# A graph network of four layers: group sums copied out of PSUM by ScalarE, and a written instruction order in the attentions

## Chip, cores and metric

The kernel runs on one core of one Trainium2 chip. The metric is the time of one execution on the device in microseconds (us). Before the change the median of three executions was 2805.52 us (2800.92 to 2822.27).

## The reference, cut to what matters

Four layers follow one another on 3327 nodes with 512 features each; an adjacency matrix of 3327 x 3327 says which node sees which. Every layer has the form x = x + layer(h, adj) with h = relu(layernorm(x)). Layers 0, 2 and 3 are graph attentions with 8 heads of 64 features:

```python
Wh = h @ W                                   # per head
e = leaky_relu(s_i[:, None] + s_j[None, :])  # two scores per node and head
e = where(adj > 0, e, NEG)
out = softmax(e) @ Wh
```

Layer 0 puts a batch norm over the nodes and a relu behind it, layers 2 and 3 an elu. Layer 1 is a SAGE layer: the mean of the neighbours' h, two products with weights that are combined, a relu.

## The kernel before

**Tiling.** Nodes are padded to 26 blocks of 128. A setup (0 to about 405 us) reads the adjacency, projects for layer 0 and builds, for each of 52 groups of 64 target nodes, the list of source nodes that any of them sees. The matrix is sparse, and lists have fixed lengths (CAPS): 22, 15, 13 chunks of 128 source rows for the first groups, 5 for 21 of the last. There are 359 chunks in all.

**A projection** writes one table row per node: for each head the 64 projected features times the exponential of the source's score, that exponential itself as a 65th column, and eight more columns with the exponential of the score times -0.8. The target's factor goes to r_dram. A leaky-relu softmax then needs no exponential per edge: its weight is the maximum of a target's and a source's factor (mx), times the 0/1 mask (wgt), and the 65th column gives the softmax's sum.

**An attention** (attend, L1000) goes through the groups in units of two or three chunks, 135 units a layer. For a unit:

- GpSimd gathers the chunks' rows by an indirect DMA each (L995) into rows, which has six buffers of one unit.
- In layer 0 alone, VectorE takes the adjacency bits of the group out of the rows (on, L1058), and ScalarE makes the mask of them (L1064), which the later layers use again.
- VectorE computes mx in PSUM (L1067) from r_bc, the group's factors spread over the partitions by TensorE (L1024), and the gathered columns; then wgt in SBUF (L1074, three buffers).
- TensorE multiplies wgt with the rows, head by head, into facc, one PSUM bank with two buffers (L1086). Four heads lie side by side on each half of the partitions.

When a group's last unit is through, group_end (L1027) divides by the sums: VectorE takes a reciprocal for each half of the partitions (rd, L1041), reading PSUM, and ScalarE does eight multiplications out of PSUM (L1044) into fhp, or in layer 0 into bn_y. After two groups a block of 128 nodes is whole. In layers 2 and 3 finish() (L1110) then loads x (fin_x), ScalarE takes an exponential and subtracts one, VectorE does two operations (L1118, L1119), and the result goes out by a DMA on ScalarE's queue (L1120).

**Beside an attention** other work goes on, a step at each tick(), called once a unit behind the unit's matmuls. Layer 0 has beside(): products of SAGE weights, and later a matmul per block for the batch norm's mean. Layer 2 has the projection of layer 3 (class Following): norm() makes the layer norm of a finished block in three steps on ScalarE and VectorE; rest() has four steps with transposes, score products (p_sd), the feature product (p_wh), exponentials, and writes to r_dram and the table. Its PSUM has one bank in layer 2, which transposes, p_sd and p_wh use in turn. The SAGE layer drives the same class for layer 2, with two banks. Layer 3 starts when the whole table of layer 3 is written.

**What sets the order.** The kernel is written in Tile: the program gives tiles, buffers and dependences, and a planner orders the instructions of each engine by the time at which its own cost model says that they are ready, with the program's order as priority. [...] The program puts group_end one unit (LATE) behind a group's last unit; where its instructions come to stand is the planner's choice.

Of the kernel before, what the change touches and what calls it, by code (L numbers as in the profile page):

```python
# [29 lines left out]
AF = mybir.ActivationFunctionType  # L30
ALU = mybir.AluOpType
AX = mybir.AxisListType
PSUM = bass.MemoryType.PSUM
# [21 lines left out]
UNIT = 3  # L55
LATE = 1
SUNIT = 2
SROWS = 8
SAHEAD = 2
RB = 2  # L60
SMALL = 53.0
# [584 lines left out]
class Following:  # L646
# [51 lines left out]
    def rest(self, c, hx):  # L698
# [15 lines left out]
        nc.scalar.activation(V[:, :, F : F + 1], sd[:, :H].rearrange("p (h o) -> p h o", o=1), AF.Exp)  # L714
        nc.scalar.activation(row[:, H * (F + 1) :], sd[:, :H], AF.Exp, scale=-0.8, bias=self.cs["down"])  # L715

        rr = pp.tile([H, P], F32, name="r_row", tag="r_row", bufs=2)
        nc.vector.tensor_scalar(rr, sd[:H, P : 2 * P], -SMALL, SMALL, ALU.max, ALU.min)  # L718
        yield True
        wh = self.psum.tile([P, D], F32, name="p_wh", tag="p_ps", bufs=self.pb)  # L720
        for kc in range(KC):
            nc.tensor.matmul(wh, hT[:, kc, :], self.Wt[:, kc, :], start=(kc == 0), stop=(kc == KC - 1))  # L722
        nc.scalar.activation(rr, rr, AF.Exp, scale=0.8, bias=self.cs["down"][:H])
        n = P // GB
        nc.sync.dma_start(
            self.r_dram[c * n : (c + 1) * n, :, :].rearrange("g h i -> h g i"), rr.rearrange("h (g i) -> h g i", i=GB)
        )
        yield True
        for h in range(H):
# [237 lines left out]
def sparse(ctx: ExitStack, tc: tile.TileContext, t: dict, out: bass.AP, WA, ls, cs, idx, rdeg, first):  # L967
# [32 lines left out]
    def attend(layer, table, r_dram, finish, tick=lambda: None, home=None):  # L1000
# [6 lines left out]
        for g in range(ls.G):  # L1007
            mine = list(ls.batches(g, UNIT))
            units += [(g, k0, n, i == 0, i == len(mine) - 1) for i, (k0, n) in enumerate(mine)]
        late = []  # L1010
        with tc.tile_pool(name=f"fatt{layer}", bufs=2) as ap, tc.tile_pool(
            name=f"facc_ps{layer}", bufs=2, space=PSUM
        ) as aps:
            hps, rbs, accs = {}, {}, {}

            def spread(g):


                if g >= ls.G:
                    return  # L1020
                rr = ap.tile([1, H * GB], F32, name="r_one", tag="r_one", bufs=3)
                nc.sync.dma_start(rr, r_dram[g : g + 1, :, :].rearrange("g h i -> g (h i)"))
                rb = aps.tile([P, H * GB], F32, name="r_bc", tag="r_bc", bufs=RB)
                nc.tensor.matmul(rb, ones[0:1, :], rr, start=True, stop=True)  # L1024
                rbs[g] = rb.rearrange("p (h i) -> p h i", i=GB)

            def group_end(g):  # L1027
                b, u = divmod(g, PG)
                if u == 0:
                    if home is None:  # L1030
                        hp_ = ap.tile([P, D], F32, name="fhp", tag="hp", bufs=2)
                        hps[b] = hp_
                    else:
                        hps[b] = home[:, b, :]
                hp, acc = hps[b], accs.pop(g)
                o0 = u * GB
                for v in range(PG):
                    src = acc[v * GB : (v + 1) * GB, : H // PG * (F + 1)].rearrange("p (q x) -> p q x", x=F + 1)
                    rd_ = ap.tile([P, H // PG, 1], F32, name="rd", tag="rd", bufs=4)
                    rd = rd_[v * GB : (v + 1) * GB]  # L1040
                    nc.vector.reciprocal(rd, src[:, :, F : F + 1])  # L1041
                    for q in range(H // PG):
                        h = q * PG + v
                        nc.scalar.mul(hp[o0 : o0 + GB, h * F : (h + 1) * F], src[:, q, 0:F], rd[:, q, :])  # L1044
                if u == PG - 1:
                    finish(b, hps.pop(b), ap)

            spread(0)
            for at, (g, k0, n, begins, ends) in enumerate(units):
                gi = ap.tile([P, UNIT, width], I32, name="rows", tag="rows", bufs=6)  # L1050
                gt = gi.bitcast(F32)
                for k in range(n):
                    gather(gi[:, k, :], table, k0 + k)
                mk = mask[:, k0 : k0 + n, :]
                if layer == 0:
                    nw = GB // WB
                    on = ap.tile([P, UNIT, nw, WB], U16, name="on", tag="on")
                    nc.vector.tensor_tensor(  # L1058
                        on[:, :n],
                        gi[:, :n, ROW:].bitcast(U16)[:, :, g * nw : (g + 1) * nw].unsqueeze(3).to_broadcast([P, n, nw, WB]),  # L1060
                        cs["bit"].unsqueeze(1).unsqueeze(1).to_broadcast([P, n, nw, WB]),
                        ALU.bitwise_and,
                    )
                    nc.scalar.activation(mk, on[:, :n].rearrange("p k w b -> p k (w b)"), AF.Sign)  # L1064
                full = [P, n, H, GB]
# [8 lines left out]
                nc.vector.tensor_tensor(wt[:, :n], mx[:, :n], mk.unsqueeze(2).to_broadcast(full), ALU.mult)  # L1074
                if ends:
                    spread(g + 1)
                if begins:
                    acc = aps.tile([P, BANK], F32, name="facc", tag="acc")
                    accs[g] = acc

                for k in range(n):
                    f, l = begins and k == 0, ends and k == n - 1
                    for q in range(H // PG):
                        for v in range(PG):
# [5 lines left out]
                                start=(f and q == 0),  # L1090
                                stop=(l and q == H // PG - 1),
                            )
                if ends:
                    late.append((at + LATE, g))
                tick()
                while late and late[0][0] <= at:
                    group_end(late.pop(0)[1])
            for _, g in late:
                group_end(g)

# [8 lines left out]
    def elu_into(xin, dst, then=lambda c, xt: None):  # L1109
        def finish(c, hp, pool):  # L1110
            k = used(c) if dst is out else P
            xr = pool.tile([P, D], F32, name="fin_x", tag="fin_x", bufs=4)
            nc.sync.dma_start(xr, xin[c * P : (c + 1) * P, :])
            ex = pool.tile([P, D], F32, name="fin_e", tag="fin_e", bufs=2)
            nc.scalar.activation(ex, hp, AF.Exp)

            nc.scalar.activation(xr, xr, AF.Identity, bias=cs["less"])
            nc.vector.scalar_tensor_tensor(xr, hp, 0.0, xr, ALU.max, ALU.add)  # L1118
            nc.vector.scalar_tensor_tensor(xr, ex, 1.0, xr, ALU.min, ALU.add)  # L1119
            nc.scalar.dma_start(dst[c * P : c * P + k, :], xr[:k, :])  # L1120
            then(c, xr)

        return finish
# [6 lines left out]
    with ExitStack() as mx:  # L1130
# [48 lines left out]
        with tc.tile_pool(name="beside", bufs=1) as wp, tc.tile_pool(name="beside_ps", bufs=1, space=PSUM) as wps:  # L1179
            bg = beside(wp, wps)  # L1180
            attend(0, *first, lambda c, hp, pool: whole.append(c), lambda: next(bg, None), y)
            for _ in bg:
# [232 lines left out]
```

## Time and profile before

| what | before |
|---|---|
| median of three executions | 2805.52 us |
| profiled execution, its own time | 2822.36 us |
| its span, first to last instruction | 2820.1 us |
| TensorE busy, granted clock | 76%, 0.804 |
| VectorE busy | 64% |
| ScalarE busy | 38% |
| GpSimd busy | 49% |
| layer 0's attention, about | 405 to 993 us |
| batch norm and SAGE layer | 993 to 1657 us |
| layer 2's attention | 1657 to 2258 us |
| layer 3's attention | 2258 to 2820 us |

In lines of the profile PE is TensorE, PEld its weight loads, DVE VectorE, ACT ScalarE, POOL GpSimd, SP the queue that issues most plain DMAs. A group of instructions has the line, the engine, the operation, output and inputs with their shapes, how often, then busy time in us and mean ns of one, and the idle time just before them with what ended it. A line of a timeline has the start in us, the duration, the instruction, and in brackets the idle time before it. The ends of matmuls are modelled. A second profiled execution would differ by some us, as the times above do.

### The profile page before, as it was taken

The page shows a single profiled execution, that of the slowest core. Times are in us where ns is not written, and L with a number is a line of the kernel's source. Part 1 is how long each engine was busy: PE and PEld are TensorE (multiplying, and loading weights), DVE is VectorE, ACT ScalarE, POOL GpSimd, SP SyncE. Part 2 cuts the span into 40 slices and gives each one's busy share as a digit, 9 for nine tenths or more (in the row PEclk, how much of TensorE's full clock was granted, in tenths as well). Part 3 has the DMA queues.
Part 4 walks back from the last instruction along what each step waited for, and adds up shares of the span by engine and source line. Part 5 has one row for each costly group of instructions (what it writes and reads, how often), then busy time and mean ns, then how long its engine had stood idle before and what let it go on. Part 6 is the DMA issues. An engine that isn't in the chain of part 4 may idle for free.

```text
span 2820.1 us, 55572 instructions
## 1 busy us (share of the span) xinstructions
PE 2134.5 (76%) x22046; PEld 1334.3 (47%) x22046; DVE 1805.2 (64%) x2233; ACT 1069.0 (38%) x3909; POOL 1383.0 (49%) x1462
## 2 busy tenths in 40 slices
PE   1888427766778759899999966788898767676775
PEld 1555214445555524333444435555655455555554
DVE  7332967778888767001111149888788488898886
ACT  3776201222223333134555522455566511122332
POOL 0000025555655401577766537666555177567562
PEclk9888767877676779999999987888899856667565
DMA  8664047866766537577877658777677277678663
GB/s 305 244 217 146 20 132 231 258 192 198 227 197 210 158 114 237 169 233 243 258 238 232 203 152 233 221 206 226 190 206 209 76 224 227 187 218 233 190 197 109
DMA packets 186638, 561.53 MB, mean 199 GB/s; under 512 B 35385, under 2 KB 40321, under 8 KB 183044
## 3 DMA queue, kind: packets, MB, share of 16 engines
q0 software_dynamic: 114880, 404.47, 49.0%
q1 hardware_dynamic: 63446, 139.40, 14.0%
q10 hardware_dynamic: 8046, 14.03, 1.4%
q8 instruction: 177, 2.90, 0.4%
q14 instruction: 89, 0.73, 0.1%
HBM read 498.42 MB, written 59.36 MB: 198 GB/s over the span
## 4 chain that ended last, share of the span: by engine, by line
PE 38%; DVE 17%; DMA 12%; issue 8%; POOL 6%; ACT 5%; DVEq 0%; POOLq 0%; SPq 0%; ACTq 0%
PE facc L1086 12%; DMA rows<-table,idx 8%; DVE wgt L1074 7%; DVE mx L1067 6%; PE p_wh L722 6%; POOL rows L995 6%; PE sage_acc L1316 5%; PE r_bc L1024 4%; PE n_ps L1265 3%; PE s_ps L1240 3%; DMA z_rows<-h_dram,idx 2%; PE p_sd L711 2%; PE p_sd L709 1%; DMA fin_x<-fx 1%; ACT v_row L730 1%
## 5 line engine op out<-in xcount | busy, mean ns | idle before, releaser
L995 POOL DMA_INDIRECT rows<-table,idx x1077 | 1035.3, 961 | 1057.3 <-SPq L1411 348.3
L1086 PE MATMUL facc<-rows,wgt 128*64 128x65 f32 x17232 | 814.7, 271 | 380.3 <-DVE rd L1041 167.9
L1086 PEld LDWEIGHTS facc<-rows,wgt 128*64 128x64 f32 x17232 | 753.8, 182 | 615.5 <-DVE wgt L1074 214.2
L1067 DVE TENSOR_TENSOR mx<-r_bc,rows 128x1536 f32<-128x1536 f32 (+1 forms) x405 | 640.5, 1581 | 52.1 <-DMA rows<-table,idx 43.8
L1074 DVE TENSOR_TENSOR wgt<-mx,mask 128x1536 f32<-128x1536 f32 (+1 forms) x405 | 634.6, 1567 | 7.1
L995 POOL DMA_INDIRECT z_rows<-h_dram,idx x359 | 341.2, 950 | 302.4 <-ACT hT L1237 147.8
L1044 ACT ACTIVATE fhp<-facc,rd 64x64 f32<-64x64 f32 x832 | 192.8, 302 | 411.9 <-DVE rd L1041 410.2
L1024 PE MATMUL r_bc<-r_one,fones 1*128 1x512 f32 x312 | 227.6, 817 | 24.8 <-DVE mx L1067 11.9
L1316 PE MATMUL sage_acc<-z_rows,z_mask 128*64 128x512 f32 x718 | 206.1, 619 | 22.6 <-DMA z_rows<-h_dram,idx 21.2
L722 PE MATMUL p_wh<-fWt,hT 128*128 128x512 f32 x416 | 206.8, 638 | 1.9 <-DVE r_row L718 1.9
L1064 ACT ACTIVATE mask<-on 128x192 uint8<-128x192 uint16 (+1 forms) x135 | 46.5, 345 | 324.8 <-DVE on L1058 324.8
L1044 ACT ACTIVATE bn_y<-facc,rd 64x64 f32<-64x64 f32 x416 | 94.5, 302 | 187.2 <-DVE rd L1041 187.2
L1270 DVE TENSOR_TENSOR s_o<-n_ps,bn_y 128x512 f32<-128x512 f32 x26 | 18.0, 692 | 223.5 <-PE n_ps L1265 223.5
L1041 DVE RECIPROCAL rd<-facc 64x4 f32<-64x4 f32 x312 | 55.4, 177 | 151.6 <-PE facc L1086 121.0
L590 PE MATMUL wh_ps<-fWt,hT 128*128 128x512 f32 x208 | 122.8, 716 | 2.8 <-ACT hT L776 2.8
L722 PEld LDWEIGHTS p_wh<-fWt,hT 128*128 128x128 f32 x416 | 79.1, 201 | 96.7 <-issue 90.5
L730 ACT ACTIVATE v_row<-p_wh,v_row 128x64 f32<-128x64 f32 x416 | 92.6, 326 | 81.7 <-PE p_wh L722 81.2
L718 DVE TENSOR_SCALAR r_row<-p_sd 8x128 f32<-8x128 f32 x52 | 14.4, 277 | 157.8 <-ACT v_row L715 154.9
L1316 PEld LDWEIGHTS sage_acc<-z_rows,z_mask 128*64 128x64 f32 x718 | 50.4, 138 | 133.1 <-issue 84.3
L1265 PE MATMUL n_ps<-fWx,aT 128*128 128x512 f32 x208 | 97.7, 606 | 0.3
L1240 PE MATMUL s_ps<-fWx,hT 128*128 128x512 f32 x208 | 94.8, 609 | 2.4 <-ACT hT L1237 2.4
L855 ACT ACTIVATE adj_s<-adj_b 128x3328 bf16<-128x3328 bf16 x26 | 77.6, 2985 | 49.1 <-DVE ok L496 45.8
(194 smaller groups left out, 2121.9 us busy)
## 6 DMA issues: line engine op xcount, KB each, us to landing
adj_i<-in_adj SPq DMA_DIRECT2D x26, 1664.0 KB
table<-v_row SPq DMA_DIRECT2D x78, 264.0 KB
rows<-table,idx POOLq DMA_INDIRECT x1077
fin_x<-fx SPq DMA_DIRECT2D x52, 256.0 KB
ln_x<-in_x SPq DMA_DIRECT2D x26, 256.0 KB
bn_x<-in_x SPq DMA_DIRECT2D x13, 512.0 KB
fx<-bn_x SPq DMA_DIRECT2D x13, 512.0 KB
fsage_x<-fx SPq DMA_DIRECT2D x26, 256.0 KB
```

The source lines that it names most:

```text
L590: nc.tensor.matmul(wh, hT[:, kc, :], self.Wt[:, kc, :], start=(kc == 0), stop=(kc == KC - 1))
L722: nc.tensor.matmul(wh, hT[:, kc, :], self.Wt[:, kc, :], start=(kc == 0), stop=(kc == KC - 1))
L730: nc.scalar.mul(V[:, h, 0:F], wh[:, h * F : (h + 1) * F], V[:, h, F : F + 1])
L995: nc.gpsimd.indirect_dma_start(out=dst, out_offset=None, in_=src[:, :], in_offset=bass.IndirectOffsetOnAxis(ap=idx[:, k : k + 1], axis=0))
L1024: nc.tensor.matmul(rb, ones[0:1, :], rr, start=True, stop=True)
L1044: nc.scalar.mul(hp[o0 : o0 + GB, h * F : (h + 1) * F], src[:, q, 0:F], rd[:, q, :])
L1067: nc.vector.tensor_tensor(mx[:, :n], rbs[g].unsqueeze(1).to_broadcast(full), gt[:, :n, H * (F + 1) : ROW].unsqueeze(3).to_broadcast(full), ...
L1074: nc.vector.tensor_tensor(wt[:, :n], mx[:, :n], mk.unsqueeze(2).to_broadcast(full), ALU.mult)
L1086: nc.tensor.matmul(accs[g][v * GB : (v + 1) * GB, q * (F + 1) : (q + 1) * (F + 1)], wt[:, k, h, :], gt[:, k, h * (F + 1) : (h + 1) * (F + 1)],
L1240: nc.tensor.matmul(ps, hT[:, kc, :], Wx[:, 0, kc, :], start=(kc == 0), stop=(kc == KC - 1))
L1265: nc.tensor.matmul(ps, aT[:, kc, :], Wx[:, 1, kc, :], start=(kc == 0), stop=(kc == KC - 1))
L1316: nc.tensor.matmul(acc[u * GB : (u + 1) * GB, :], m, z, start=f, stop=l)
```

## The change

Within an attention, TensorE, VectorE and ScalarE keep the order in which the program is written (tc.manual_schedule); GpSimd and SP are still planned. The program is rewritten for that:

- The gathers of unit i+1, and in layer 0 its on and mask, are written behind wgt of unit i (load).
- The end of a group is a generator, ending(g), of which later() takes a step per unit: ScalarE copies the sums of both halves, 128 x 260, from PSUM to SBUF; a unit later VectorE takes one reciprocal of 128 x 4 and ScalarE multiplies, now out of SBUF; after a block's second group the steps of finish() follow, a unit each.
- tick() is called in later(), ahead of the unit's matmuls.
- r_one, the row of a group's factors, is fetched two groups ahead (fetch); r_bc is made ahead of the matmuls of a group's last unit.
- The result of a block goes out on SP's queue instead of ScalarE's.
- In Following.rest the exponentials join the step with p_sd, and r_row the step with p_wh. This holds for the SAGE layer too.

```diff
@@ rest @@
         nc.scalar.activation(row[:, H * (F + 1) :], sd[:, :H], AF.Exp, scale=-0.8, bias=self.cs["down"])
+        yield True
 
         rr = pp.tile([H, P], F32, name="r_row", tag="r_row", bufs=2)
         nc.vector.tensor_scalar(rr, sd[:H, P : 2 * P], -SMALL, SMALL, ALU.max, ALU.min)
-        yield True
         wh = self.psum.tile([P, D], F32, name="p_wh", tag="p_ps", bufs=self.pb)
         for kc in range(KC):
             nc.tensor.matmul(wh, hT[:, kc, :], self.Wt[:, kc, :], start=(kc == 0), stop=(kc == KC - 1))
+        yield True
         nc.scalar.activation(rr, rr, AF.Exp, scale=0.8, bias=self.cs["down"][:H])
...
-        yield True
         for h in range(H):
@@ attend @@
-        ) as aps:
-            hps, rbs, accs = {}, {}, {}
+        ) as aps, tc.manual_schedule(engines={ET.PE, ET.DVE, ET.Activation}):
+            rows, rrs, rbs, accs, ends = {}, {}, {}, {}, []
+
+            def fetch(g):
+                if g < ls.G:
+                    rr = ap.tile([1, H * GB], F32, name="r_one", tag="r_one", bufs=3)
+                    nc.sync.dma_start(rr, r_dram[g : g + 1, :, :].rearrange("g h i -> g (h i)"))
+                    rrs[g] = rr
...
-            def group_end(g):
+            def ending(g, hps={}):
...
-                hp, acc = hps[b], accs.pop(g)
-                o0 = u * GB
+                hp, o0 = hps[b], u * GB
+                fin = finish(b, hp, ap)
+                if u == PG - 1:
+                    next(fin)
+                sm = ap.tile([P, sw], F32, name="sums", tag="sums", bufs=3)
+                nc.scalar.copy(sm, accs.pop(g)[:, :sw])
+                sm = sm.rearrange("p (q x) -> p q x", x=F + 1)
+                yield
+                rd = ap.tile([P, hq, 1], F32, name="rd", tag="rd", bufs=3)
+                nc.vector.reciprocal(rd, sm[:, :, F : F + 1])
                 for v in range(PG):
-                    src = acc[v * GB : (v + 1) * GB, : H // PG * (F + 1)].rearrange("p (q x) -> p q x", x=F + 1)
-                    rd_ = ap.tile([P, H // PG, 1], F32, name="rd", tag="rd", bufs=4)
-                    rd = rd_[v * GB : (v + 1) * GB]
-                    nc.vector.reciprocal(rd, src[:, :, F : F + 1])
-                    for q in range(H // PG):
+                    mine = slice(v * GB, (v + 1) * GB)
+                    for q in range(hq):
                         h = q * PG + v
-                        nc.scalar.mul(hp[o0 : o0 + GB, h * F : (h + 1) * F], src[:, q, 0:F], rd[:, q, :])
+                        nc.scalar.mul(hp[o0 : o0 + GB, h * F : (h + 1) * F], sm[mine, q, 0:F], rd[mine, q, :])
+                yield
                 if u == PG - 1:
-                    finish(b, hps.pop(b), ap)
-
+                    del hps[b]
+                    yield from fin
+
+            def later():
+                for e in list(ends):
+                    if next(e, 0) == 0:
+                        ends.remove(e)
+                tick()
...
+            load(0)
+            for i, (g, k0, n, begins, stops) in enumerate(units):
+                gt = rows.pop(i)
...
                 nc.vector.tensor_tensor(wt[:, :n], mx[:, :n], mk.unsqueeze(2).to_broadcast(full), ALU.mult)
-                if ends:
-                    spread(g + 1)
+                load(i + 1)
+                later()
                 if begins:
+                    fetch(g + 2)
                     acc = aps.tile([P, BANK], F32, name="facc", tag="acc")
                     accs[g] = acc
+                if stops:
+                    spread(g + 1)
...
-                if ends:
-                    late.append((at + LATE, g))
-                tick()
-                while late and late[0][0] <= at:
-                    group_end(late.pop(0)[1])
-            for _, g in late:
-                group_end(g)
+                if stops:
+                    ends.append(ending(g))
+            while ends:
+                later()
@@ elu_into @@
             ex = pool.tile([P, D], F32, name="fin_e", tag="fin_e", bufs=2)
+            yield
             nc.scalar.activation(ex, hp, AF.Exp)
 
             nc.scalar.activation(xr, xr, AF.Identity, bias=cs["less"])
+            yield
             nc.vector.scalar_tensor_tensor(xr, hp, 0.0, xr, ALU.max, ALU.add)
             nc.vector.scalar_tensor_tensor(xr, ex, 1.0, xr, ALU.min, ALU.add)
-            nc.scalar.dma_start(dst[c * P : c * P + k, :], xr[:k, :])
+            nc.sync.dma_start(dst[c * P : c * P + k, :], xr[:k, :])
             then(c, xr)
```

## The prediction

> **What bounds the kernel now.** I read the page's engine shares and slices first, then the busy time of each stage, then VectorE's waits in the three attentions, then single stretches of its timeline.
>
> ```profile
> PE 2134.5 (76%) x22046; PEld 1334.3 (47%) x22046; DVE 1805.2 (64%) x2233; ACT 1069.0 (38%) x3909; POOL 1383.0 (49%) x1462
> DVE  7332967778888767001111149888788488898886
> PEclk9888767877676779999999987888899856667565
> ```
>
> No engine is full over the span, but slices 5 to 14 and 24 to 40, the attentions, have VectorE at 7 to 9 tenths. By stage (layer 0, layer 2, layer 3; columns as in the first line):
>
> ```profile
> core 0: us, PE busy (x) PEld busy (x) DVE busy (x) ACT busy (x) POOL busy (x), PEclk, DMA share, GB/s
> 405.00:993.00 588.00, 428.93 (x5978) 296.78 (x5978) 468.96 (x513) 148.03 (x569) 334.67 (x353) 0.72 0.69 212
> 1657.00:2258.00 601.00, 482.50 (x6583) 333.72 (x6581) 484.73 (x532) 303.63 (x1197) 344.60 (x358) 0.86 0.68 198
> 2258.00:2820.00 562.00, 384.13 (x5848) 306.01 (x5848) 468.38 (x426) 129.74 (x468) 348.58 (x359) 0.62 0.68 199
> ```
>
> VectorE is busy 469 of 588, 485 of 601 and 468 of 562 us: it is the nearest bound, and idles 119, 116 and 94 us. TensorE's clock is 0.6 to 0.7 in layers 0 and 3. Two groups of instructions are the body:
>
> ```profile
> L1067 DVE TENSOR_TENSOR mx<-r_bc,rows 128x1536 f32<-128x1536 f32 (+1 forms) x405 | 640.5, 1581 | 52.1 <-DMA rows<-table,idx 43.8
> L1074 DVE TENSOR_TENSOR wgt<-mx,mask 128x1536 f32<-128x1536 f32 (+1 forms) x405 | 634.6, 1567 | 7.1
> L1041 DVE RECIPROCAL rd<-facc 64x4 f32<-64x4 f32 x312 | 55.4, 177 | 151.6 <-PE facc L1086 121.0
> ```
>
> The body hardly waits; the reciprocal of a group's sums waits 152 us. VectorE's waits in layer 0, then 2, then 3 (total us, times, longest):
>
> ```profile
> DVE on L1058 <- DMA rows<-table,idx: 69.8, 36, 11.3
> DVE rd L1041 <- PE facc L1086: 47.3, 26, 4.0
> ...
> DVE r_row L718 <- ACT v_row L715: 21.4, 11, 3.7
> DVE rd L1041 <- ACT fhp L1044: 20.4, 17, 3.2
> DVE rd L1041 <- PE facc L1086: 16.5, 15, 2.5
> DVE fin_x L1118 <- ACT fhp L1044: 13.3, 9, 2.4
> ...
> DVE rd L1041 <- PE facc L1086: 57.2, 35, 2.6
> ```
>
> One group's end in layer 3, and one wait of layer 0:
>
> ```profile
> 2496.73 1.77 DVE L1067 TENSOR_TENSOR mx<-r_bc,rows 128x1536 f32<-128x1536 f32 x1
> 2500.27 0.17 DVE L1041 RECIPROCAL rd<-facc 64x4 f32<-64x4 f32 x1 [1.78 <-PE facc L1086]
> 2500.37 1.72 DVE L1074 TENSOR_TENSOR wgt<-mx,mask 128x1536 f32<-128x1536 f32 x1
> ...
> 2498.22 2.00 PE L1086 MATMUL facc<-rows,wgt 128*64 128x65 f32 x32
> 2502.37 2.87 PE L1086 MATMUL facc<-rows,wgt 128*64 128x65 f32 x48 [2.15 <-DVE rd L1041]
> ...
> 648.11 0.36 DVE L1058 TENSOR_TENSOR on<-rows,fbit 128x192 uint16<-128x192 uint16 x1 [3.50 <-DMA rows<-table,idx]
> ```
>
> The planner put the reciprocal between the next unit's mx and wgt. VectorE stops there for the group's last matmuls (2498.22 to 2500.2); TensorE then has nothing until that wgt is done, 2.15 us. Each waits for the other once a group, [...] 32 of these matmuls take 2.00 us here, 1.15 us elsewhere. In layer 0, counting units in order, the L1058 at 648.11 belongs to the unit whose mx starts at 657.51: the planner placed it two to three units early, so VectorE waits for a gather not yet needed, and six buffers of rows give a lead of about three.
>
> [...]
>
> **The change part by part.**
>
> *The floor.* A layer has 135 units, 89 of three rows and 46 of two; mx plus wgt take 3.60 and 2.53 us start to start where nothing holds them (1667.53 to 1671.13; 2494.20 to 2496.73): 89 x 3.60 + 46 x 2.53 = 437 us. One reciprocal a group at 0.18: 9. Layer 3 adds two L1118/L1119 a block, 26 x 1.2 = 31, its start (8 to the first mx) and end (20 from the last wgt): 505. Layer 2 adds 19 for r_row and the norm, starts in 7 and ends in 39: 542. Layer 0 adds 33 for L1058, no L1118, 2 and 7: 488. The room is 562 - 505 = 57, 601 - 542 = 59 and 588 - 488 = 100 us.
>
> *Group end.* ScalarE copies 128x260 out of PSUM a unit after the group, VectorE's reciprocal comes a unit later. Copy: between 278 ns (128x128) and 587 (128x512), 0.38 by the line; 156 make 60 us of ScalarE, hidden where it has room (busy 148, 304, 130 us). [...] Two reciprocals of 0.34 together become one of 0.11 to 0.18: 52 x 0.16 = 8 us a layer saved, on the path. The accumulator is free after the copy, not after eight multiplications. The waits for facc (47, 17, 57 us) go unless TensorE is over a unit late; next late is then the gather.
>
> *Loading a unit ahead.* L1058 of unit i+1 now follows wgt of i, so it asks for rows that the next mx needs anyway. GpSimd's gathers keep their sequence; it starts one each 1.25 us if free, 359 x 1.25 = 449 us, under all three floors by 39 or more. Of the 70 us I let 30 stay: landing takes 4 to 8 us after issue, early gathers beside the weight loads more.
>
> *Projection.* Ticks move ahead of the unit's matmuls; rest() puts the exponentials with p_sd and r_row with p_wh. In layer 2 p_wh (3.7 us) now stands ahead of a unit's matmuls, three wgt buffers cover that; uncovered it costs up to 26 x 3.7 = 96. In the SAGE layer, bound by TensorE, I take 0, bounds -5 to +10.
>
> *Queues.* The 52 results go out from SP instead of ScalarE's queue, 0.34 us of issue each. On SP they wait for VectorE, and behind them stand r_one (now fetched two groups early), fin_x loads and the table writes: 0, up to 10 if a fin_x comes late. Mean matmuls of layer 0 a tick later, hp and rd buffers, one r_bc more explicit: 0.
>
> *Written order.* [...] behind a copy stand masks, multiplications and the norm, for which VectorE waits a unit later. Entering and leaving three regions: 0 to 15, I take 5.
>
> *Sum.* Layer 0 recovers 70 of 100, layer 3 43 of 57 (both have an idle ScalarE), layer 2 only 22 of 59[...]. 135 - 5 = **130 us**. The profiled execution took 2822.4 us (span 2820.1), so 2692 for one like it; the median of before, 2805.5, is 17 lower: **2675**.
>
> **Rivals.**
>
> *Gathers take the place.* For it: the three engines' needs lie within 10% of each other, and DMA is at 0.68 already. Layer 0 moves 212 x 588 = 125 MB; at the 225 GB/s that similar stretches reach on average it needs 554 us, a gain of 34; layers 2 and 3 then give 10 to 15 each. 2805 - 60 = 2745. Against: stretches at 240 GB/s, and gathers held mostly by TensorE's late release (180 us).
>
> *ScalarE in order, slower than before.* In layer 2 hT stands in the same tick as its transposes, the exponentials with p_sd. TensorE reaches a tick's transposes after the earlier unit, with p_wh, r_bc and 48 matmuls 3.7 + 1.1 + 1.6 = 6.4 us. If that is handed on to VectorE once a block, 26 x 6.4 = 166 us are added in layer 2, against 110 gained elsewhere: 2861. [...] Against: the copy for which VectorE waits needs later matmuls anyway.
>
> *Nothing much happens:* the waits reappear as wgt buffers or rows: 2800.
>
> **Chances.** Forecast, 60 to 200 us off: 0.62. Gathers, 10 to 60 off: 0.17. Over 200 off: 0.03. Nothing: 0.04. Slower: 0.14. About 1%, 28 us, is what a measurement of this kernel can tell from none. About a third of the gathers' case (0.05) lies below 28 off: faster 0.62 + 0.12 + 0.03 = 0.77, same 0.05 + 0.04 = 0.09, slower 0.14. The range, 2600 to 2795, takes forecast and gathers, 0.8.
>
> **What would show it.** The reciprocal's wait under 20 us in all; L1058 waiting under 40; VectorE over 90% in layer 3's middle; TensorE's clock there above 0.62; layers at about 518, 579 and 519 us. I am wrong if VectorE then waits for ScalarE in layer 2 by over 100 us, or if rows are waited for as long as facc was.

## The result, and the profile after

The changed kernel takes 2829.03 us (median of 18 executions, 2822.80 to 2837.72), the kernel before 2810.78 us (18 executions): a ratio of 1.0072, 95% interval 1.0050 to 1.0093. The forecast was 2675 us; the range ended at 2795. The profiled execution after took 2825.3 us (span 2823.0), so it lies 3 us above the one before. Its four stages (layer 0, batch norm and SAGE, layer 2, layer 3), with the columns of the page's first part, then TensorE's clock, DMA share and GB/s:

```profile
405.00:925.00 520.00, 390.87 (x5978) 264.21 (x5978) 455.28 (x459) 172.90 (x617) 332.83 (x352) 0.82 0.77 238
925.00:1590.00 665.00, 603.27 (x2134) 254.57 (x2132) 164.17 (x362) 296.72 (x1069) 342.38 (x362) 0.97 0.67 208
1590.00:2270.00 680.00, 503.95 (x6582) 343.56 (x6582) 480.68 (x480) 328.02 (x1249) 343.38 (x357) 0.83 0.60 174
2270.00:2823.00 553.00, 374.70 (x5848) 294.02 (x5848) 462.75 (x374) 160.53 (x520) 347.10 (x359) 0.65 0.70 202
```

Layer 0 went from 588 to 520 us, the SAGE stage stayed (664, 665), layer 3 went from 562 to 553, and layer 2 rose from 601 to 680: -68 + 1 + 79 - 9 = +3. VectorE's work is 4 to 14 us less than before in each attention; its idle time fell from 119 to 65 us in layer 0 and from 94 to 90 in layer 3, and rose from 116 to 199 in layer 2. The groups of instructions that answer to those shown of before:

```profile
L1093 DVE TENSOR_TENSOR mx<-r_bc,rows 128x1536 f32<-128x1536 f32 (+1 forms) x405 | 639.9, 1580 | 271.9 <-PE r_bc L1027 219.5
L1100 DVE TENSOR_TENSOR wgt<-mx,mask 128x1536 f32<-128x1536 f32 (+1 forms) x405 | 638.2, 1576 | 28.3
L1047 DVE RECIPROCAL rd<-sums 128x4 f32<-128x4 f32 x156 | 26.5, 170 | 4.9 <-ACT sums L1043 4.9
```

The reciprocal's 152 us of waiting became 5. In their place mx, which had waited 52 us, now waits 272, and 219.5 of them for r_bc, the spread of a group's factors by TensorE. VectorE's waits by layer (0, then 2, then 3; total us, times, longest):

```profile
DVE mx L1093 <- PE r_bc L1027: 42.7, 27, 4.3
DVE on L1079 <- DMA rows<-table,idx: 12.4, 1, 12.4
...
DVE mx L1093 <- PE r_bc L1027: 125.3, 39, 7.0
DVE mx L1093 <- DMA rows<-table,idx: 24.6, 3, 18.7
...
DVE mx L1093 <- PE r_bc L1027: 51.6, 36, 2.4
DVE mx L1093 <- DMA rows<-table,idx: 23.2, 2, 22.7
```

How r_bc comes late is seen at one group's end in layer 3 (VectorE's timeline, then TensorE's):

```profile
2492.48 1.22 DVE L1100 TENSOR_TENSOR wgt<-mx,mask 128x1024 f32<-128x1024 f32 x1
2493.74 1.23 DVE L1093 TENSOR_TENSOR mx<-r_bc,rows 128x1024 f32<-128x1024 f32 x1
2495.08 1.23 DVE L1100 TENSOR_TENSOR wgt<-mx,mask 128x1024 f32<-128x1024 f32 x1
2497.80 1.77 DVE L1093 TENSOR_TENSOR mx<-r_bc,rows 128x1536 f32<-128x1536 f32 x1 [1.50 <-PE r_bc L1027]
...
2493.76 2.00 PE L1115 MATMUL facc<-rows,wgt 128*64 128x65 f32 x32 [0.81 <-DVE wgt L1100]
2495.69 2.07 PE L1027 MATMUL r_bc<-r_one,fones 1*128 1x512 f32 x2
```

r_bc stands ahead of the matmuls of a group's last unit, but behind those of the unit before it. These can only start when that unit's wgt is done, here at 2493.70 (2492.48 + 1.22). From there TensorE needs 2.00 us for 32 multiplications and 2.07 for r_bc, 4.07 in all; VectorE has one unit of two rows to do in the meantime, 2.57 us, and then stops. In the kernel before, the trace shows r_bc finished 8.5 to 9.8 us ahead of the mx that reads it (medians of the 51 later groups of each layer; 10th percentile 5 to 8 us, never under 4.1). After, the median is 0.0, and 125 of 153 groups have less than 0.3 us. The planner had moved r_bc forward by about two units, as much as a whole group of five chunks; the written order holds it where the program has it.

In layer 2 the projection's p_wh is in the same queue, ahead of the unit's matmuls. It shares its one PSUM bank with p_sd, so it is itself held for VectorE's r_row of the same step, which reads p_sd:

```profile
2002.75 0.27 DVE L718 TENSOR_SCALAR r_row<-p_sd 8x128 f32<-8x128 f32 x1
...
2011.11 1.77 DVE L1093 TENSOR_TENSOR mx<-r_bc,rows 128x1536 f32<-128x1536 f32 x1 [3.94 <-PE r_bc L1027]
...
2003.07 5.40 PE L721 MATMUL p_wh<-fWt,hT 128*128 128x512 f32 x8 [2.46 <-DVE r_row L718]
2008.40 1.62 PE L1115 MATMUL facc<-rows,wgt 128*64 128x65 f32 x48
2009.95 1.12 PE L1027 MATMUL r_bc<-r_one,fones 1*128 1x512 f32 x2
```

TensorE idles 2.46 us until r_row is there, then does 5.40 + 1.62 + 1.12 us before VectorE gets its r_bc. VectorE's wait of 3.94 us is what is left of that. Counted over layer 2, 22 of the 39 waits for r_bc, 100 of the 125 us, have a p_wh among TensorE's work since the wgt before last; another 19 us have other parts of the projection there. In layer 0, 26 of the 43 us have work of beside() in that place.

### The profile page after: what moved, and what is told of

Its sections match the earlier page's. It is cut to its first block, busy times and chain, and to the rows that moved or that the text cites. A ratio compares the mean times of both kernels' runs of the same rounds, so it can differ in the third digit from the quotient of the medians.

```text
span 2823.0 us, 55457 instructions
## 1 busy us (share of the span) xinstructions
PE 2103.1 (74%) x22046; PEld 1296.9 (46%) x22046; DVE 1782.9 (63%) x2077; ACT 1149.3 (41%) x4065; POOL 1379.8 (49%) x1462
## 4 chain that ended last, share of the span: by engine, by line
PE 32%; DVE 13%; DMA 8%; issue 6%; ACT 4%; POOL 4%; DVEq 0%; POOLq 0%; SPq 0%; ACTq 0%
PE p_wh L721 7%; PE facc L1115 7%; DVE mx L1093 6%; PE sage_acc L1350 5%; DMA rows<-table,idx 5%; DVE wgt L1100 4%; POOL rows L994 3%; PE r_bc L1027 3%; PE n_ps L1299 3%; DMA z_rows<-h_dram,idx 2%; PE s_ps L1274 2%; ACT fhp L1052 1%; PE p_sd L710 1%; PE p_sd L708 1%; POOL z_rows L994 1%
## 5 line engine op out<-in xcount | busy, mean ns | idle before, releaser
L1115 PE MATMUL facc<-rows,wgt 128*64 128x65 f32 x17232 | 772.0, 262 | 377.7 <-DVE wgt L1100 224.8
L1115 PEld LDWEIGHTS facc<-rows,wgt 128*64 128x64 f32 x17232 | 711.2, 173 | 631.0 <-DVE wgt L1100 303.8
L1093 DVE TENSOR_TENSOR mx<-r_bc,rows 128x1536 f32<-128x1536 f32 (+1 forms) x405 | 639.9, 1580 | 271.9 <-PE r_bc L1027 219.5
L1052 ACT ACTIVATE fhp<-sums,rd 64x64 f32<-64x64 f32 x832 | 219.8, 334 | 426.1 <-DVE rd L1047 418.4
L721 PE MATMUL p_wh<-fWt,hT 128*128 128x512 f32 x416 | 226.6, 696 | 49.7 <-DVE rs_h L633 27.5
L721 PEld LDWEIGHTS p_wh<-fWt,hT 128*128 128x128 f32 x416 | 87.7, 220 | 162.9 <-issue 109.0
L1043 ACT COPY sums<-facc 128x260 f32<-128x260 f32 x156 | 56.7, 364 | 245.6 <-PE facc L1115 166.6
L1052 ACT ACTIVATE bn_y<-sums,rd 64x64 f32<-64x64 f32 x416 | 109.5, 333 | 4.1 <-DVE rd L1047 2.2
```

What stands on the lines that cost most here:

```text
L1052: nc.scalar.mul(hp[o0 : o0 + GB, h * F : (h + 1) * F], sm[mine, q, 0:F], rd[mine, q, :])
L1093: nc.vector.tensor_tensor(mx[:, :n], rbs[g].unsqueeze(1).to_broadcast(full), gt[:, :n, H * (F + 1) : ROW].unsqueeze(3).to_broadcast(full), ...
L1115: nc.tensor.matmul(accs[g][v * GB : (v + 1) * GB, q * (F + 1) : (q + 1) * (F + 1)], wt[:, k, h, :], gt[:, k, h * (F + 1) : (h + 1) * (F + 1)],
```

## The experiments

The runs fell on chips that differ: on those of the result and of the third set below the kernel before takes 2811 and 2816 us, on the four others 3142 to 3169. Each run is therefore given as a ratio to the kernel before on its own chip, and layers are compared on one kind of chip only. For one kernel, a layer still differs by up to 17 us between two of the four slower chips. The table has the length of an attention from its first mx to its last wgt, off the timelines:

| kernel | ratio, 95% interval | layer 0 | layer 2 | layer 3 |
|---|---|---|---|---|
| *chips at 2811 and 2816 us* | | | | |
| before | 1 | 579 | 555 | 534 |
| changed | 1.0072, 1.0050 to 1.0093 | 512 | 627 | 522 |
| both edits (early r_bc, projection behind) | 0.9413, 0.9370 to 0.9455 | 469 | 527 | 476 |
| both edits, pauses of before in rest() | 0.9734, 0.9692 to 0.9777 | 469 | 614 | 476 |
| both edits, p_sd in two steps | 0.9574, 0.9535 to 0.9614 | 469 | 529 | 475 |
| changed, one r_bc for all groups | 0.9442, 0.9402 to 0.9483 | 470 | 543 | 476 |
| *chips at 3142 to 3169 us* | | | | |
| before | 1 | 623 | 660 | 633 |
| changed | 0.9841, 0.9818 to 0.9863 | 578 | 674 | 588 |
| early r_bc | 0.9654, 0.9632 to 0.9676 | 570 | 627 | 568 |
| projection behind | 0.9836, 0.9803 to 0.9869 | 575 | 653 | 582 |
| both edits | 0.9590, 0.9570 to 0.9610 | 569 | 608 | 567 |
| both edits, more slack | 0.9761, 0.9737 to 0.9785 | 568 | 672 | 574 |
| both edits, no copy of sums | 0.9601, 0.9575 to 0.9626 | 572 | 616 | 577 |
| changed program, planned | 0.9981, 0.9963 to 0.9998 | 643 | 651 | 589 |

### First set: the two places in TensorE's order, and the order itself

Early r_bc, for a group's successor ahead of the group's first matmuls:

```diff
                     accs[g] = acc
-                if stops:
-                    spread(g + 1)
+                    spread(g + 1)
```

> The changed kernel, with the broadcast r_bc of a group's successor issued ahead of the matmuls of the group's first unit (it stood ahead of those of its last unit). Theory A, r_bc is late only by its place in TensorE's order: VectorE's wait of mx for r_bc, 43, 125 and 52 us in layers 0, 2 and 3 of the changed kernel, falls below 10 us in each, and the time falls by about 150 to 220 us, to some 2610 to 2680 us. Theory B, in layer 2 TensorE is late with everything because p_wh stands in the written order ahead of a unit's matmuls and is held for r_row: r_bc's wait goes, but wgt or mx then waits for matmuls (the three buffers of wgt run out); layer 2 keeps at least 650 us of its 680 and the time falls by 40 to 90 us, to 2740 to 2790 us.

Measured: 0.9654. The wait for r_bc fell to 7, 9 and 2 us, as theory A has it, and layer 2 did not stay long. But the gain over the changed kernel (0.9841 on such a chip) is 0.019, or 59 us, not 150 to 220: in layers 0 and 3 VectorE waited for sums (58 and 63 us at the reciprocal) and, for 10 and 20 us, at wgt instead. The same kernel on two more chips:

> The changed kernel with r_bc ahead of its predecessor's first matmuls, and nothing else moved. On a chip on which the kernel before takes about 2811 us: if the place of r_bc is the whole loss, layers 0, 2 and 3 come to within 10 us of those with both edits (469, 527 and 476 us from the first mx to the last wgt; the changed kernel 512, 627 and 522) and the ratio to the kernel before is 0.94 to 0.945. If the projection's parts ahead of the matmuls cost by themselves, layers 0 and 3 do so and layer 2 stays at 550 us or more: 0.95 to 0.965. On a slow chip: 0.965, as before.

> r_bc ahead of its predecessor's first matmuls, and nothing else moved. On a chip on which the kernel before takes about 2811 us: if the place of r_bc is the whole loss, 0.94 to 0.945 and layers 0, 2 and 3 within 10 us of 469, 527 and 476 us (first mx to last wgt); if the projection's parts ahead of the matmuls cost by themselves, layers 0 and 3 do so and layer 2 stays at 550 us or more: 0.95 to 0.965. On a slow chip a third 0.965.

Measured: 0.9655 (0.9628 to 0.9682) and 0.9623 (0.9590 to 0.9655), both on the slow kind. What the early r_bc alone gives on a chip like the first stays unmeasured.

Projection and endings behind the unit's matmuls:

```diff
                 load(i + 1)
-                later()
...
+                later()
                 if stops:
                     ends.append(ending(g))
```

> The changed kernel, with the step that issues a unit's endings and the projection's parts moved behind the unit's matmuls on TensorE's list (r_bc keeps its place ahead of the last unit's matmuls). Theory A: r_bc stays late in layers 0 and 3 and those stages keep their times within 10 us; layer 2 gains what p_wh cost r_bc, some 20 to 50 us, so 2780 to 2810 us. Theory B: p_wh was what kept TensorE late in layer 2; layer 2 falls from 680 to 610 us or less and the time to 2760 us or less.

> The changed kernel with endings and projection's parts behind the unit's matmuls, r_bc left ahead of the last unit's. On a chip like the first: layers 0 and 3 stay within 8 us of the changed kernel's 512 and 522 us (no projection there); layer 2 falls from 627 to 560 to 590 us: ratio 0.985 to 0.995. If p_wh alone made r_bc late in layer 2, it falls to 540 us or less.

Measured: 0.9836 and 0.9850 (0.9817 to 0.9884), against the changed kernel's 0.9841. Alone this edit gives nothing that can be measured. In layers 0 and 3 r_bc stays about as late as in the changed kernel on another slow chip (70 and 52 us on the first chip, 78 and 50 on the second, for 73 and 45). In layer 2 the wait for it falls to 53 and 47 us, for 154: most of it came from what this edit moves. But layer 2 is only 21 and 7 us shorter, no more than two such chips can differ by, for VectorE now waits for ScalarE instead: ahead of r_row 43 and 48 us, where the changed kernel has 5, and ahead of rs_h over 20.

> Both edits: r_bc ahead of a group's first matmuls, endings and the projection's parts behind a unit's matmuls. Theory A: within 15 us of the early r_bc alone. Theory B: faster than the early r_bc alone by at least 40 us, all of it in layer 2.

Measured: 0.9590 beside the early r_bc's 0.9654 on the same chip, 19 us more, of them 18 in layer 2. That is more than theory A allowed and half of what theory B asked. The projection's place counts once r_bc is out of its way.

The program without the written order (manual_schedule left out of attend's pools):

> The changed kernel's program without the written order: the planner orders TensorE, VectorE and ScalarE in the attentions as in the kernel before, so only the rewritten program (sums copied by ScalarE, one reciprocal, masks and gathers a unit ahead, endings in three steps) is left of the change. Theory A, the order of r_bc is the loss: the planner moves r_bc ahead, its wait is under 10 us a layer, and the time is 2680 to 2750 us. Rival, the copy and the split endings themselves cost: 2820 us or more, with r_bc's wait gone.

> The changed kernel's program without the written order, left to the planner. On a chip like the first: if the copy and the work a unit ahead free VectorE by themselves, 0.96 or less; if VectorE now waits for the copy where it waited for facc, 0.99 to 1.01 (0.998 on a slow chip, where it waited for sums 43, 76 and 108 us in layers 0, 2 and 3).

> The changed program left to the planner. On a chip like the first: 0.99 to 1.01 if VectorE waits for the copy of the sums where it waited for facc, as on the slow chips (0.998, 0.994); 0.96 or less if the copy and the work a unit ahead free VectorE by themselves.

Measured: 0.9981, 0.9940 (0.9919 to 0.9961) and 0.9952 (0.9938 to 0.9966), with next to no wait for r_bc. The rewritten program without its order is worth 0.2 to 0.6% on these slow chips. Its groups of instructions show the old waits again: 238 us ahead of the reciprocal, for 378 in the kernel before on such a chip, and 129 us ahead of on, for 62:

```profile
L1047 DVE RECIPROCAL rd<-sums 128x4 f32<-128x4 f32 x156 | 27.6, 177 | 238.0 <-ACT sums L1043 172.5 <-issue 62.8 <-ACT fin_x L1144 2.4
L1079 DVE TENSOR_TENSOR on<-rows,fbit 128x192 uint16<-128x192 uint16 (+1 forms) x135 | 45.1, 334 | 128.7 <-DMA rows<-table,idx 126.8 <-issue 1.6
```

### Second set: the slow kind of chip, and slack

> The kernel before, for a trace beside the next three kernels on one chip. The four first variants ran on a chip on which the kernel before took 3142 us, not 2811, and on which TensorE in a unit's 48 multiplications stood still, without a recorded cause, for 417 us in the three attentions with the early r_bc (gaps over 150 ns, counted beyond 60 ns), against 11 us in the changed kernel on the first chip. Theory C, that standing still belongs to the chip: the kernel before shows over 60 us of it there. Theory D, it belongs to the order of the early r_bc: under 20 us on either chip.

> The changed kernel, on the same chip as its variants, so that their gain over it can be read. If the chip is like that of the four first variants: 3080 to 3130 us, ratio to before 0.98 to 1.0 (moving the projection's parts alone gave 0.984 there). If it is like the first: 1.00 to 1.01. VectorE's wait of mx for r_bc is again over 200 us in the three attentions.

> The early r_bc with endings and projection's parts behind the unit's matmuls, next to the kernels before and after. Theory A, the place of r_bc in the order is the loss: ratio to the kernel before at most 0.965 on either chip, and on a chip like the first 0.94 to 0.96, with VectorE over 85% busy in layers 0 and 3. Theory D: on a chip like the first TensorE stands still within units for over 100 us here too and the ratio stays at 0.97 or above.

Measured: the kernel before 3165.7 us, the changed one 0.9841, both edits 0.9612 (0.9581 to 0.9642). Within units TensorE stood still for 95 us in the kernel before, 174 in the changed one and 426 with both edits (counted where two multiplications start more than 0.15 us apart, what exceeds 0.06). The first chip has 10 and 11 by the same count, from distances of 0.16 us at most. So theory C holds: the standing still belongs to the chip. Its amount goes with the kernel, more where TensorE waits less for VectorE (ahead of facc 321 us for rd and wgt in the kernel before, 41 for wgt with both edits); why is not shown. This is a piece of its timeline in layer 3, with both edits, where multiplications come four or fewer at a time:

```profile
2705.74 0.35 PE L1113 MATMUL facc<-rows,wgt 128*64 128x65 f32 x4
2706.49 0.35 PE L1113 MATMUL facc<-rows,wgt 128*64 128x65 f32 x4 [0.41 <-issue]
2707.25 0.32 PE L1113 MATMUL facc<-rows,wgt 128*64 128x65 f32 x2 [0.41 <-issue]
2707.49 1.12 PE L1027 MATMUL r_bc<-r_one,fones 1*128 1x512 f32 x2
```

Here the changed kernel is faster than the one before, not slower, though r_bc is waited for longer in all (73, 154 and 45 us). The kernel before waits 378 us ahead of its reciprocals on this chip, against 152 on the first, so there is more to win back; 5 us of it are left in the changed kernel.

One more unit between copy and reciprocal, and a fourth wgt buffer:

```diff
                 yield
+                yield
                 rd = ap.tile([P, hq, 1], F32, name="rd", tag="rd", bufs=3)
...
-                wt = ap.tile([P, UNIT, H, GB], F32, name="wgt", tag="wgt", bufs=3)
+                wt = ap.tile([P, UNIT, H, GB], F32, name="wgt", tag="wgt", bufs=4)
```

> As the run before, with one more unit between a group's copy of sums and the reciprocal, and four wgt buffers for three: VectorE may be three units ahead of TensorE before it waits. If VectorE's waits for sums and wgt, some 60 us in layer 3 of the early r_bc alone (27 and 39 for the reciprocal, 20 for wgt), were a matter of slack: 30 to 90 us faster than the run before, most on a slow chip. If TensorE is short of throughput there, the waits come back at other places and the gain is under 15 us.

Measured: 0.9761, slower than both edits by 48 us. Layers 0 and 3 gained 7 and 4 us (on the same chip both edits have 576 and 577), so slack is not what they lack; layer 2 lost 57 (615 to 672). There VectorE waits 51 us for ScalarE ahead of rs_h and 68 ahead of r_row, for 20 and 42 with both edits. Which of the two changes does that was not separated; that the later endings push the projection's steps is likely, but not shown.

### Third set: a chip like the first

> The early r_bc with endings and projection's parts behind the unit's matmuls, again beside the next three, in the hope of a chip like that of the two first profiles (the kernel before near 2811 us). On such a chip theory A expects 0.94 to 0.96 of the kernel before, and TensorE standing still within units for under 20 us in the three attentions, where the two other chips showed 417 and 426. Theory D (the order itself makes TensorE stand still) expects over 100 us of it there, and 0.97 or more. On a chip where the kernel before takes over 3100 us: 0.955 to 0.965, as twice before.

Measured: 2648.24 us beside 2816.17, ratio 0.9413; TensorE stood still for 9 us. Theory A holds. The stages, and VectorE's waits in layers 0, 2 and 3:

```profile
404.00:886.00 482.00, 357.88 (x5945) 239.01 (x5943) 452.11 (x458) 168.90 (x601) 342.72 (x359) 0.88 0.82 262
886.00:1556.00 670.00, 609.46 (x2165) 258.33 (x2164) 164.18 (x363) 301.70 (x1084) 342.04 (x359) 0.96 0.66 206
1556.00:2140.00 584.00, 473.41 (x6584) 332.03 (x6584) 481.32 (x480) 328.09 (x1249) 342.57 (x359) 0.86 0.68 204
2140.00:2647.00 507.00, 350.40 (x5848) 283.44 (x5848) 461.74 (x374) 158.05 (x520) 343.97 (x359) 0.70 0.74 221
```

```profile
DVE on L1079 <- DMA rows<-table,idx: 12.5, 1, 12.5
DVE wgt L1100 <- PE facc L1113: 0.5, 1, 0.5
...
DVE mx L1093 <- DMA rows<-table,idx: 20.2, 2, 20.0
DVE r_row L718 <- ACT v_row L714: 15.8, 7, 3.5
...
DVE mx L1093 <- DMA rows<-table,idx: 24.9, 2, 23.9
DVE wgt L1100 <- DVE mx L1093: 0.5, 1, 0.5
```

After an attention's first gather VectorE waits for next to nothing in layers 0 and 3; it is busy 94% and 91% of those stages, and 97% from 2200 to 2600 us. At a group's end it goes straight on, since r_bc is there 4.6 to 5.5 us ahead (median):

```profile
2364.79 1.23 DVE L1100 TENSOR_TENSOR wgt<-mx,mask 128x1024 f32<-128x1024 f32 x1
2365.93 0.17 DVE L1047 RECIPROCAL rd<-sums 128x4 f32<-128x4 f32 x1
2366.05 1.23 DVE L1093 TENSOR_TENSOR mx<-r_bc,rows 128x1024 f32<-128x1024 f32 x1
2367.38 1.23 DVE L1100 TENSOR_TENSOR wgt<-mx,mask 128x1024 f32<-128x1024 f32 x1
2368.70 1.77 DVE L1093 TENSOR_TENSOR mx<-r_bc,rows 128x1536 f32<-128x1536 f32 x1
```

The pauses of rest() as in the kernel before, on top of both edits:

```diff
         nc.scalar.activation(row[:, H * (F + 1) :], sd[:, :H], AF.Exp, scale=-0.8, bias=self.cs["down"])
-        yield True
 
         rr = pp.tile([H, P], F32, name="r_row", tag="r_row", bufs=2)
         nc.vector.tensor_scalar(rr, sd[:H, P : 2 * P], -SMALL, SMALL, ALU.max, ALU.min)
+        yield True
         wh = self.psum.tile([P, D], F32, name="p_wh", tag="p_ps", bufs=self.pb)
...
-        yield True
         nc.scalar.activation(rr, rr, AF.Exp, scale=0.8, bias=self.cs["down"][:H])
...
+        yield True
         for h in range(H):
```

> As the run before, with the pauses in the projection's last part put back where the kernel before had them: r_row in the step of p_sd, p_wh in the next, the eight scalings in the one after. Only layer 2's attention and the SAGE stage change. If the moved pauses help VectorE, which then asks for p_sd a step later, layer 2 loses 15 us or more here, as VectorE waits for p_sd in the very step that TensorE computes it. If it was p_wh and r_row in one step that held TensorE: layer 2 gains 15 us or more.

Measured: 0.9734; layer 2 is 614 us for 527. VectorE's largest wait there:

```profile
DVE r_row L717 <- ACT v_row L714: 81.5, 23, 7.6
```

The moved pauses are worth 88 us with both edits. What they move is r_row, out of the step of p_sd into that of p_wh, and r_row's exponential with its write, into the step of the scalings; the exponentials of v_row stand with p_sd in both kernels, though the list of changes above has them moved. VectorE stands at r_row, with the next mx behind it, for 81.5 us in all, against 15.8 with both edits alone.

p_sd's two halves in two steps:

```diff
             nc.tensor.matmul(sd[:, :H], hT[:, kc, :], WA[:, wl, kc, H:], start=(kc == 0), stop=(kc == KC - 1))
+        yield True
         for kc in range(KC):
```

> As the first run of these four, with one more pause between the two halves of p_sd, so that no step of the projection puts more than 4 us on TensorE (p_wh, 3.9 us at 0.8 of the clock). If layer 2 is bound by bursts of the projection on TensorE, for which VectorE and ScalarE wait in order (r_row 42 us, rs_h 20 us there): layer 2 falls by 15 to 40 us. If it is bound by TensorE's sum of work (538 us busy of 673 on a slow chip): within 10 us.

Measured: 0.9574. Layer 2 did not shrink (529), and from its last wgt to layer 3's first gather it now takes 89 us instead of 48: six blocks' feature products are left over when the units end, instead of three.

One r_bc for all groups of an attention, so that all later ones are left out:

```diff
-                if g < ls.G:
+                if 0 < g < ls.G:
+                    rbs[g] = rbs[0]
+                elif g < ls.G:
```

> The changed kernel, leaving out r_bc for all groups but an attention's first, whose r_bc then serves all groups (so the attention's weights are not the reference's): VectorE never waits for r_bc, and TensorE has 102 multiplications of 0.6 to 1.2 us less in each attention, some 85 us of work. Order and all the rest are those of the changed kernel. Theory A: of the changed kernel's time the wait goes (219 us on the first chip, 273 us on the slow one), less what comes up in its place: ratio to the kernel before 0.93 to 0.96. If r_bc only stands for a TensorE that is late anyway, the wait moves on to facc, and the ratio stays at 0.97 or above.

Measured: 0.9442, inside what theory A expected. With p_wh and the endings left where the change put them, taking r_bc out brings layers 0 and 3 to the lengths of both edits (470 and 476) and layer 2 to within 16 us of it (543, 527). In layers 0 and 3 no other wait came up in its place. In layer 2 VectorE's waits for ScalarE at rs_h, r_row and rs_g rose from 9 to 47 us, so that of the 125 us some 84 came off:

```profile
DVE rs_h L633 <- ACT ln_j L685: 26.3, 21, 2.7
...
DVE r_row L718 <- ACT v_row L714: 11.6, 12, 1.9
DVE rs_g L635 <- ACT rs_y L629: 8.6, 21, 0.4
```

This run takes r_bc's multiplications off TensorE as well; both edits keep them and reach the same lengths in layers 0 and 3, so it was the waiting that cost. Together the two runs show the cause: r_bc's place, and p_wh's place mainly through r_bc.

### Fourth set: the copy

Both edits, reciprocal and scalings out of PSUM at the same steps:

```diff
-                sm = ap.tile([P, sw], F32, name="sums", tag="sums", bufs=3)
-                nc.scalar.copy(sm, accs.pop(g)[:, :sw])
+                sm = accs.pop(g)[:, :sw]
                 sm = sm.rearrange("p (q x) -> p q x", x=F + 1)
```

> Both edits, and the copy of the sums left out: reciprocal and scalings read facc in PSUM, as in the kernel before, at the same steps of the order. Compared with both edits (0.941 on a chip like the first, 0.959 to 0.961 on the slow ones). If the copy is what frees TensorE's accumulators in time: 1 to 4% slower than with it, with TensorE's first matmuls of a group waiting for the scalings of two groups before. If the unit's distance in the order does it alone: within 0.5%, or faster by up to 10 us, as ScalarE does 156 copies less at 0.36 us[...].

Measured: 0.9601, beside 0.9590 and 0.9612 with the copy on two chips of that kind. The copy, the first thing that the change's name says, makes no difference that shows there. What stays of the new group end is that VectorE asks a unit later; no run tests that alone. On a chip like the first this was not run.

## Why the prediction was wrong, step by step

**Queues: "one r_bc more explicit: 0".** This step failed. The price could be had from the trace of before: 32 multiplications 2.00 us and a two-row unit of VectorE 2.53, both in the prediction, and r_bc 2.07 us in the same stretch, where the granted clock was 0.50 (2494 to 2504 us):

```profile
2496.22 2.07 PE L1024 MATMUL r_bc<-r_one,fones 1*128 1x512 f32 x2
```

Behind the previous unit's matmuls it ends 4.1 us after that unit's wgt, 1.5 us after VectorE is ready, or 2.4 after 48 multiplications of 2.87. Layer 3 shows 36 such waits, 51.6 us in all, 1.4 each, the longest 2.4. A few us on, at a granted clock of 1.00 (2507.5 to 2510.5 us), r_bc takes 1.12 us and 32 multiplications 1.15; there the sum is under 2.53 and nothing is due: 29 of layer 3's 51 later groups read an r_bc that took over 1.6 us and wait 1.55 on average, 45 us together, and the 22 others wait 0.33. I looked for what the program adds and removes and took r_bc, which it only keeps, for unmoved. But the written order takes away the planner's move too, and the trace of before shows that move: 4 us and more between r_bc and its reader.

**Group end: "next late is then the gather".** The first half held (152 us became 5), the second did not: next late was r_bc. Rows are waited for hardly more than once per layer, at its start.

**Projection: "three wgt buffers cover that; uncovered it costs up to 26 x 3.7 = 96".** This step failed too, and costs more. The cover was real for wgt and not asked of r_bc, which has no buffer's lead in this order. Its 96 us for the uncovered case are about the size of what came: 100 of VectorE's 125 us of waiting in layer 2 have p_wh in the way, held for r_row and then 3.7 to 6.5 us long (10th to 90th percentile). Moving rest()'s pauses was priced at nothing in an attention; with both edits it saves 88 us (614 against 527), and what it saves in the changed kernel was not run.

**The floor** was right for layers 0 and 3. Forecast from VectorE's own work: 488, 542 and 505 us a stage. Both edits measure 482, 584 and 507. VectorE is the bound in layers 0 and 3; in layer 2 its floor is not reached, with VectorE at 481 and TensorE at 473 of 584 us. One reading is loose: of the slices called 7 to 9 tenths, four have 4 or 6. The sums by stage, on which the floor rests, do not use it.

**Loading a unit ahead** was right: L1058's wait fell from 70 to 12 us (30 forecast), and layer 0 landed at 520 (518 forecast), though by luck, as two errors cancel: 43 us lost to r_bc, and more recovered than I allowed. In the kernel before, the 36 L1058 that wait for rows start 4.1 to 8.2 us after the issue of their unit's last gather: a median of 6.8 for the nine up to 470 us, with weight loads issued beside them until 458, and 4.7 for the later ones.

**Prices.** The copy takes 0.364 us (0.38). The one reciprocal takes 170 ns; the 0.11 us at the low end of its range was an estimate that no trace shows. The multiplications take 334 ns out of SBUF, 302 out of PSUM in the kernel before: 32 ns more. With both edits VectorE's waits show neither the copy nor these.

**Sum.** Of 135 us, layer 0 gave 68 of 70, layer 3 only 9 of 43, and layer 2 -79 instead of +22. The 22 was my estimate; ScalarE's busy time rose there from 304 to 328 us. With both edits the stages give 106, 55 and 17, and SAGE -6: 172 us, so that for a kernel that makes r_bc in time 130 was low, mostly by layer 0.

**The rivals.** "Gathers take the place" fell: with both edits the transfers reach 262 GB/s in layer 0, beyond the 225 that I took as a limit. "ScalarE in order" named the right layer and the right sign, and the wrong engine: VectorE waits for ScalarE in layer 2's stage for 37 us, 13 of them at r_row, and for TensorE's r_bc 125. "Nothing much happens" came nearest in time (2800, chance 0.04), but not by its mechanism: wgt was not waited for and rows hardly more than at each layer's start, and terms of both signs happened to cancel. The signs promised (reciprocal under 20, L1058 under 40, clock of layer 3 above 0.62: 5, 12, 0.65) all came true without the time following, and neither sign of being wrong appeared. Those that failed were VectorE over 90% in layer 3's middle (88% from 2350 to 2750 us; 97% with both edits, 2200 to 2600), the one that measures the bound, and the lengths of layers 2 and 3.

## What to carry to other kernels

When a written order replaces a planner's, list every producer whose result is read at a step's start, with its slack in the trace of before: those with slack may have it from the planner, as r_bc had, and they are what the order must place by hand. Place each behind work that is finished a unit earlier than its reader asks, not merely ahead of the unit in the text; here one line moved, with a second for the projection, turns +0.7% into -5.9%. Judge by the wait ahead of the bound engine's main operation, since a named wait that vanishes may have only changed its name.

## What was not expected of the hardware

The kernel before takes 3142 to 3169 us on four chips and 2811 and 2816 on two: one program, some 12% apart. The SAGE stage, which the change touches only by the pauses of rest(), takes 664 to 670 us on the chips of the one sort and 764 to 778 on the others. On the slow ones single engines stand with nothing in the trace that releases them. With both edits TensorE loses 426 us so in the attentions (9 on a fast chip), mostly in stops of 0.3 to 1.1 us, more than half of them after four multiplications or fewer; ScalarE is held for longer, 9.45 us at a time in this piece of the chain of waits of the kernel before, from its SAGE stage there:

```profile
1226.83 0.30 ACT z_mask L1297
1227.12 9.45 another core or an unknown queue
...
1236.65 0.30 ACT z_mask L1297
1236.95 9.45 another core or an unknown queue
```

Such waits of unknown origin make up 184 us of the chain of that run; the traces of the fast chips have none. Their cause stays open. It follows that the sign of a change can depend on the chip: the changed kernel is 0.7% slower on one sort and 1.6% faster on the other, while both edits gain on each.

TensorE's clock also costs on the new path. r_bc's two multiplications take over 1.6 us, mostly 2.07, in 30 of layer 3's groups, and 1.12 in most of layer 2's. At 2495.69 in the timelines above r_bc takes 2.07 us and the granted clock was 0.50 (2495.7 to 2497.8 us); at 2009.95 it takes 1.12, at 1.00. The mean clock was 0.65 in layer 3's stage and 0.83 in layer 2's. In the kernel before, layer 3 has a mean clock of 0.64 from 2296 to 2800 us, and TensorE's longest pause there is 3.13 us, most are about 2. What lowers the clock is not shown, so it stays open whether an engine that waits makes what it is waited for longer.
